# A Mamba-2 and ternary FFN kernel on one Trainium2 core: the total of a chunk's running sums comes from their last column by way of DRAM, and the sums from s on become a difference

## The chip, the cores and the metric

The kernel runs on one core of one Trainium2 chip. The metric is device time in microseconds. The kernel before took 1155.3 us, the median of three runs (1153.39 to 1156.26).

The engines work side by side, each in the order of its own instructions, and meet at semaphores: TensorE (PE; its weight loads are listed as PEld), VectorE (DVE), ScalarE (ACT), GpSimd (POOL) and SyncE (SP), which here only issues DMAs. PE multiplies a stationary operand (the weights) with a moving one and writes into PSUM; DVE and ACT read PSUM, DMAs and POOL work on SBUF.

## The reference

Sixteen sequences of 512 tokens with 256 features go through a Mamba-2 block and a feed-forward block with ternary weights, each with layer norms and residuals. The change touches the scan of the Mamba-2 block:

```python
dt = jax.nn.softplus(dt + dt_bias)
A = -jnp.exp(A_log)
dA = jnp.exp(dt * A)
xdt = xh * dt[..., None]
def step(S, inp):
    dA_t, xdt_t, B_t, C_t = inp
    S = dA_t[:, :, None, None] * S + xdt_t[..., None] * B_t[:, None, None, :]
    y_t = jnp.einsum('bhpn,bn->bhp', S, C_t)
    return (S, y_t)
_, y = lax.scan(step, S0, ...)
y = y.transpose(1, 0, 2, 3) + D[None, None, :, None] * xh
y = y.reshape(b, l, D_INNER)
y = y * jax.nn.silu(z)
y = y * lax.rsqrt(jnp.mean(y * y, axis=-1, keepdims=True) + 1e-05) * norm_w
return y @ out_proj_w.T
```

There are 8 heads of 64 values and a state of 128 for each value. The decay of a head over a stretch of tokens is the exponential of the sum of `a = dt * A` over them, so the scan can be cut into chunks once these sums are known.

## The kernel before

**Tiling.** A sequence is cut into 4 chunks of 128 tokens. 4 chunks times 8 heads give 32 columns, `W = 32`. `a` is a tile of 128 tokens x 32 columns.

**Stages of one sequence.** `stage_a` projects the input, does the convolution and the activations (`pm` on PE, L296; `cv` on ACT, L301, and DVE, L303; the silu, L308; `pz`, L318). `stage_a0` and `stage_t0` norm the input of a sequence ahead and transpose it to `x1T` (L273, L276). `stage_a2` computes softplus and `a` on DVE (L420 to L438) and calls `sums_of`. `stage_r` loads `mt` (the running sums of 8 heads, spread to all partitions), `stage_s` or, for three chunks of the first sequence, `stage_s_v` forms differences of running sums (ACT L538, DVE L525), `stage_b1` takes their exponentials (L549). `stage_b0` makes the decays `dec` and `ecum` (L473, L478), `stage_d` loads `ct` spread to all partitions, `stage_e` multiplies it by C (POOL L499). `stage_b2` walks over the chunks: `prepare` transposes x into `px` (L588), multiplies by dt (`xdt`, DVE L590), forms B C products (`pg`, L594 to L597), multiplies `mt` (L606) and makes `xend` on POOL (L603); then come the state `pst` (L623, L629), `py` (L637, L644) and `y` (L656, L660). `stage_c1` and `stage_c2` are the output projection (L709) and the feed-forward block (`ph` L755, gelu L761, `pf` L789, `o` L795).

**The sums.** `sums_of` makes, in one PSUM tile `pd`, three products on PE. `a` under the triangle `after` gives at token s the sum over the tokens after s in its chunk; `a` under `ones` gives the sum over the whole chunk, in every partition (both L449, outputs 128 x 32). `a` as weights against the triangle `incl` gives the running sums with the 32 columns as partitions and the tokens along the row (L450, output 32 x 128). ACT copies the running sums to `cum` (L454); DVE copies the other two to `sums` (L455), whose first half is the sum after s and second half the total. `cum` goes to DRAM as `raw` (L457) and comes back spread to all partitions as `mt` (L511). PE transposes `cum` (L461) and DVE copies that to `cums` (L463), token by token the running sum up to s. In `stage_b0`, later, ACT takes the exponential of all of `sums` in one instruction: `dec[:, 0]` weighs a token into the chunk's end state (L603), `dec[:, 1]` decays the old state over a chunk (L651).

**What sets the order.** On PE, ACT, POOL and DVE the order of the code is the order of the engine. The code is written as generators that `interleave` advances by hand-set shares. Each pass of the main loop has a first `interleave` (projections of sequence i + 1, first half of the block of i - 1) and a second one (feed-forward of i - 1, chunks of i, sums and decays of i + 1). In the second, `stage_a2(i + 1)` runs at 0.08 to 0.36, `stage_r` of two chunks at 0.365, `stage_b0(i + 1)` at 0.5. For the first sequence the stages are run one after the other:

```python
for stage in (
    stage_t0(1), stage_a6(0), stage_s_v(0, 1, 2, 3), ternary(1), stage_s(0, 0), stage_b0(0),
    stage_d(0), stage_b1(0, 0),
):
    run(stage)
```

`ternary(1)` rounds a weight matrix on DVE (L206). For the second sequence `stage_b0(1)` stands at 0.9 of a longer `interleave`. SP's DMAs are placed by the scheduler of the framework. Tiles are taken from pools with a fixed number of buffers: `pd` is in `ps_tr` (2 banks of PSUM), `sums` in `small` (3), DRAM tiles in `dram` (2). `ps_a` has 4 banks; its buffers go round `pm`, `pz`, `px`, `pst`, `py`.

Of the kernel before, what the change touches and what calls it, by code (L numbers as in the profile page):

```python
# [28 lines left out]
F32 = mybir.dt.float32  # L29
BF16 = mybir.dt.bfloat16  # L30
AF = mybir.ActivationFunctionType
ALU = mybir.AluOpType
# [3 lines left out]
P = 128  # L36
# [24 lines left out]
def mamba_ffn_kernel(  # L61
# [17 lines left out]
    nc = tc.nc  # L79
    NB = x.shape[0]  # L80

    const = ctx.enter_context(tc.tile_pool(name="const", bufs=1))
# [7 lines left out]
    dram = ctx.enter_context(tc.tile_pool(name="dram", bufs=2, space=bass.MemoryType.DRAM))  # L90
# [6 lines left out]
    def load_x(b):  # L97
# [9 lines left out]
    ones = const.tile([P, P], F32)  # L107
    nc.gpsimd.memset(ones, 1.0)
    incl = const.tile([P, P], F32)
    nc.gpsimd.affine_select(  # L110
        out=incl, in_=ones, compare_op=ALU.is_ge, fill=0.0, base=0,
        pattern=[[1, P]], channel_multiplier=-1,
    )
    after = const.tile([P, P], F32)
    nc.gpsimd.affine_select(
        out=after, in_=ones, compare_op=ALU.is_gt, fill=0.0, base=0,
        pattern=[[-1, P]], channel_multiplier=1,
    )
    mhalf = const.tile([P, NC], F32)
    nc.gpsimd.memset(mhalf, -0.5)  # L120
# [292 lines left out]
    def stage_a2(b):  # L413


        W = NC * NH
        dt, neg, sil = seqs[b]["dt"], seqs[b].pop("neg"), seqs[b].pop("sil")
        df = dt.rearrange("p c h -> p (c h)")
        z = small.tile([P, W], F32, tag="sp_z", name=f"sp_z_{b}", bufs=1)
        nc.vector.scalar_tensor_tensor(z, neg, 2.0, sil, ALU.mult, ALU.subtract)  # L420
        nc.vector.reciprocal(z, z)
        nc.vector.tensor_mul(z, z, sil)
        e = small.tile([P, W], F32, tag="sp_e", name=f"sp_e_{b}", bufs=1)
        nc.vector.tensor_mul(e, z, z)
        yield 0.15
        acc = small.tile([P, W], F32, tag="sp_a", name=f"sp_a_{b}", bufs=1)
        nc.vector.tensor_scalar_mul(acc, e, ATANH[0])
        for k in ATANH[1:3]:
            nc.vector.scalar_tensor_tensor(acc, acc, k, e, ALU.add, ALU.mult)
        yield 0.15  # L430
        for k in ATANH[3:]:
            nc.vector.scalar_tensor_tensor(acc, acc, k, e, ALU.add, ALU.mult)
        yield 0.15
        nc.vector.scalar_tensor_tensor(acc, acc, 1.0, z, ALU.add, ALU.mult)
        nc.vector.tensor_scalar_max(df, df, 0.0)
        nc.vector.scalar_tensor_tensor(df, acc, 2.0, df, ALU.mult, ALU.add)
        a = small.tile([P, NC, NH], F32, tag="a", name=f"a_{b}")
        nc.vector.tensor_tensor(a, dt, negA.unsqueeze(1).to_broadcast([P, NC, NH]), ALU.mult)  # L438
        yield 0.25
        yield from sums_of(b, a)  # L440

    def sums_of(b, a):


        W = NC * NH
        af = a.rearrange("p c h -> p (c h)")
        pd = ps_tr.tile([P, 512], F32, tag="tr", name=f"pd_{b}")
        for i, tri in enumerate((after, ones)):
            nc.tensor.matmul(pd[:, i * W : (i + 1) * W], tri, af, start=True, stop=True)  # L449
        nc.tensor.matmul(pd[0:W, 2 * W : 2 * W + P], af, incl, start=True, stop=True)  # L450
        sums = small.tile([P, 2, W], F32, tag="sums", name=f"sums_{b}")
        pc = pd[0:W, 2 * W : 2 * W + P]
        cum = small.tile([W, P], F32, tag="cum", name=f"cum_{b}", bufs=1)
        nc.scalar.copy(cum, pc)  # L454
        nc.vector.tensor_copy(sums.rearrange("p i w -> p (i w)"), pd[:, 0 : 2 * W])  # L455
        raw = dram.tile([W, P], F32, tag="raw", name=f"raw_{b}")
        nc.sync.dma_start(raw, cum)  # L457
        seqs[b].update(sums=sums, cum=cum, raw=raw)
        yield 0.15
        turned = pd[:, 2 * W + P : 3 * W + P]  # L460
        nc.tensor.transpose(turned, cum, ident[0:W, 0:W])  # L461
        cums = small.tile([P, W], F32, tag="cums", name=f"cums_{b}", bufs=2)
        nc.vector.tensor_copy(cums, turned)  # L463
        seqs[b].update(cums=cums)
        yield 0.15


    def stage_b0(b):


        s = seqs[b]
        s["dec"] = small.tile([P, 2, NC, NH], F32, tag="dec", name=f"dec_{b}")
        nc.scalar.activation(  # L473
            s["dec"].rearrange("p i c h -> p (i c h)"), s["sums"].rearrange("p i w -> p (i w)"),
            AF.Exp,
        )
        ecum = small.tile([NC * NH, P], F32, tag="ecum", name=f"ecum_{b}", bufs=1)
        nc.scalar.activation(ecum, s.pop("cum"), AF.Exp)  # L478
        s["way"] = dram.tile([NC * NH, P], F32, tag="way", name=f"way_{b}")
        nc.sync.dma_start(s["way"], ecum)  # L480
        yield 0.1
# [370 lines left out]
    with tc.manual_schedule(engines=ordered):  # L852
# [10 lines left out]
# [5 lines that stand above are left out]
# [13 lines left out]
            (stage_t0(2), T0_WORK, 0.81, 0.83),  # L881
            (stage_a6(1), 0.1, 0.84, 0.841),
            (stage_b0(1), 0.1, 0.9, 0.901),
            (stage_b1(1, 0, 1), 0.2, 0.902, 0.903),
            (stage_s(1, 2), 1.0, 0.92, 0.95),
# [3 lines left out]
        for i in range(1, NB - 1):  # L889
# [11 lines left out]
                (stage_r(i + 1, 0, 1), 0.2, 0.365, 0.37),  # L901
                (stage_s(i + 1, 0), 1.0, 0.44, 0.49),
                (stage_b0(i + 1), 0.1, 0.5, 0.51),
                (stage_b1(i + 1, 0), 0.1, 0.515, 0.52),
                (stage_s(i + 1, 1), 1.0, 0.53, 0.61),
# [70 lines left out]
```

## Time and profile before

| what | value |
|---|---|
| median of the runs | 1155.3 us |
| the profiled execution | 1156.0 us, of it the span of the instructions 1154.3 us |
| PE busy | 1090.4 us, 94% of the span |
| DVE, ACT, POOL busy | 824.8, 696.4, 588.9 us |
| granted TensorE clock | 0.977 of full speed on average |
| products L449 in the whole run | 64 instructions, 276 ns median each as the profile models them |
| copy of the sums L455 (DVE) | 16, 218 ns |
| `raw` to DRAM, `mt` back | 16 and 64 DMAs, 1.4 and 4.0 us to land |

The profile is one execution. Busy times of PE overlap in part, since matmuls are pipelined; the chain of waits, which follows the work that ended last back to the start, counts each stretch of time once. Its rows give start, length and what; those of the timeline give start, length, engine, line, operation and tiles, with the idle time before in brackets.

### The profile page before, as it was taken

What the parts mean: (1) busy time and instruction counts of PE and PEld (TensorE: products, weight loads), DVE (VectorE), ACT (ScalarE), POOL (GpSimd) and SP (SyncE); (2) the same over time, 40 slices, a digit from 0 to 9 for tenths busy, and PEclk for the clock granted to TensorE, in tenths of its full rate; (3) what the DMA queues carried; (4) which work ended last, traced back from release to release, by engine and by line L of the source; (5) the groups of instructions that cost most, each with busy time, mean ns of one, the idle gap of its engine ahead of it and who ended that gap; (6) DMA issues with size and microseconds to landing.
All of it is one profiled execution on the core that took longest, in us unless ns stands there. A gap on an engine that the chain in (4) does not pass through costs nothing.

```text
span 1154.3 us, 17172 instructions
## 1 busy us (share of the span) xinstructions
PE 1090.4 (94%) x6052; PEld 715.6 (62%) x6052; DVE 824.8 (71%) x2137; ACT 696.4 (60%) x1378; POOL 588.9 (51%) x699
## 2 busy tenths in 40 slices
PE   5787799999999999999999999999999999999897
PEld 2344367575766757576675757667575766757575
DVE  4674867769686776968677695867779586776652
ACT  5628465676666567666656766665675666566321
POOL 1243635646463564646356464635646463565842
PEclk9788899999999999999999999999999999999899
DMA  6312012220312222031222203122220312212000
GB/s 197 124 58 77 18 62 86 74 93 19 130 37 67 82 74 92 19 130 37 70 79 74 93 19 130 37 73 76 74 93 19 130 37 74 75 56 92 1 10 28
DMA packets 34534, 81.23 MB, mean 70 GB/s; under 512 B 4368, under 2 KB 23440, under 8 KB 32400
## 3 DMA queue, kind: packets, MB, share of 16 engines
q1 hardware_dynamic: 32896, 79.97, 20.0%
q8 instruction: 48, 0.79, 0.3%
q10 hardware_dynamic: 1552, 0.16, 0.1%
q14 instruction: 38, 0.31, 0.1%
HBM read 71.21 MB, written 8.91 MB: 69 GB/s over the span
## 4 chain that ended last, share of the span: by engine, by line
PE 56%; POOL 17%; DVE 15%; ACT 9%; issue 2%; DMA 1%; POOLq 0%; ACTq 0%; DVEq 0%
PE pf L789 19%; PE ph L755 12%; POOL ct L499 9%; PE py L637 5%; PE pm L296 5%; DVE cv L303 4%; PE pst L623 4%; ACT mt L538 4%; PE py L644 3%; POOL x3p L743 3%; DVE st_f L224 2%; DVE x L695 2%; ACT mt L549 2%; ACT cv L301 2%; POOL xend L603 1%
## 5 line engine op out<-in xcount | busy, mean ns | idle before, releaser
L303 DVE SCALAR_TENSOR_TENSOR cv<-pm,cw_sb,cv 128x511 f32<-128x511 f32 (+2 forms) x288 | 215.3, 748 | 75.5 <-ACT cv L301 68.3
L789 PE MATMUL pf<-w_sb,hT 128*128 128x256 f32 x1024 | 238.0, 382 | 0.0
L789 PEld LDWEIGHTS pf<-w_sb,hT 128*128 128x128 f32 x1024 | 190.0, 190 | 35.8 <-issue 11.5
L755 PE MATMUL ph<-x3p,w_bf 128*128 128x512 bf16 x768 | 190.5, 382 | 3.1 <-POOL x3p L743 0.7
L296 PE MATMUL pm<-x1T,win_sb 128*128 128x512 f32 x384 | 186.6, 609 | 0.3 <-ACT x1T L276 0.3
L761 ACT ACTIVATE hT<-ph,b_sb 128x512 f32<-128x512 f32 x128 | 88.0, 688 | 130.9 <-PE ph L755 130.7
L538 ACT ACTIVATE mt<-mt,cums 128x128 f32<-128x128 f32 x488 | 152.4, 388 | 0.0
L660 POOL TENSOR_TENSOR zs<-y,zs 128x512 f32<-128x512 f32 x64 | 81.4, 1272 | 108.2 <-DVE y L656 106.5
L709 PE MATMUL po<-wo_sb,zs 128*128 128x256 f32 x512 | 127.0, 393 | 4.1 <-DVE att L715 4.1
L755 PEld LDWEIGHTS <-w_bf 128*128 128x128 bf16 x768 | 70.8, 98 | 88.7 <-issue 24.1
L318 PE MATMUL pz<-x1T,win_sb 128*128 128x512 f32 x256 | 124.9, 611 | 0.7 <-ACT state L626 0.7
L709 PEld LDWEIGHTS po<-wo_sb,zs 128*128 128x128 f32 x512 | 96.9, 194 | 32.5 <-issue 14.3
L296 PEld LDWEIGHTS pm<-x1T,win_sb 128*128 128x128 f32 x384 | 71.1, 193 | 71.9 <-issue 66.1
L499 POOL TENSOR_TENSOR ct<-ct,xbc 128x1024 f32<-128x1024 f32 x48 | 113.1, 2383 | 0.0
L301 ACT ACTIVATE cv<-pm,cw_sb 128x512 f32<-128x512 f32 x96 | 65.1, 678 | 69.1 <-PE pm L296 67.8
L656 DVE SCALAR_TENSOR_TENSOR y<-xbc,dsk,py 128x128 f32<-128x128 f32 x256 | 71.3, 341 | 49.0 <-PE py L644 43.2
L568 POOL TENSOR_TENSOR y<-y 128x256 f32<-128x256 f32 x64 | 46.6, 728 | 115.3 <-ACT y L567 115.3
L637 PE MATMUL py<-mt,xdt 128*64 128x128 f32 x1024 | 95.7, 282 | 0.0
L322 ACT ACTIVATE zs<-pz 128x512 f32<-128x512 f32 x64 | 37.9, 592 | 86.4 <-PE pz L318 86.4
L231 POOL TENSOR_TENSOR rs_c<-rs_c,mhalf 128x2 f32<-128x2 f32 x32 | 25.1, 785 | 125.0 <-DVE rms L579 93.8
L318 PEld LDWEIGHTS pz<-x1T,win_sb 128*128 128x128 f32 x256 | 48.7, 196 | 58.0 <-issue 48.1
L644 PE MATMUL py<-ct,state 128*64 128x128 f32 x768 | 75.6, 276 | 6.9 <-POOL ct L499 6.9
(130 smaller groups left out, 1808.9 us busy)
## 6 DMA issues: line engine op xcount, KB each, us to landing
mt<-raw SPq DMA_DIRECT2D x64, 512.0 KB, 4.0
ct<-way SPq DMA_DIRECT2D x16, 1536.0 KB, 6.3
xin<-in_x SPq DMA_DIRECT2D x16, 512.0 KB, 3.8
out<-o SPq DMA_DIRECT2D x30, 256.0 KB, 2.2
w_in<-in_w SPq DMA_DIRECT2D x1, 1024.0 KB, 8.7
w_sb<-in_w SPq DMA_DIRECT2D x1, 1024.0 KB, 11.0
win_sb<-in_w_in SPq DMA_DIRECT2D x1, 768.0 KB, 6.0
win_sb<-in_w_in SPq DMA_DIRECT2D x1, 512.0 KB, 8.1
```

What stands on the lines that cost most here:

```text
L296: nc.tensor.matmul(pm, win_sb[:, k, DI + m * P : DI + (m + 1) * P], x1T[:, k, :], start=(k == 0), stop=(k == 1),)
L301: nc.scalar.activation(cv, pm, AF.Copy, scale=cw_sb[:, m, 3:4])
L303: nc.vector.scalar_tensor_tensor(cv[:, j:], pm[:, 0 : L - j], cw_sb[:, m, 3 - j : 4 - j], cv[:, j:], ALU.mult, ALU.add,)
L318: nc.tensor.matmul(pz, win_sb[:, k, j * P : (j + 1) * P], x1T[:, k, :], start=(k == 0), stop=(k == 1),)
L499: nc.gpsimd.tensor_tensor(ct[:, c - 1], ct[:, c - 1], xbc[:, 5, c * P : (c + 1) * P].unsqueeze(1).to_broadcast([P, NH, P]), ALU.mult,)
L538: nc.scalar.activation(mt[:, h, :], mt[:, h, :], AF.Relu, bias=s["cums"][:, c * NH + h : c * NH + h + 1], scale=-1.0,)
L637: nc.tensor.matmul(py[h % 2 * HD : (h % 2 + 1) * HD, j, :], xdt[:, h * HD : (h + 1) * HD], mts[c][:, h, :], start=True, stop=(c == 0),)
L644: nc.tensor.matmul(py[h % 2 * HD : (h % 2 + 1) * HD, j, :], state[:, h * HD : (h + 1) * HD], ct[:, c - 1, h, :], start=False, stop=True,)
L709: nc.tensor.matmul(po[:, 0:DM], g[:, k, c * P : (c + 1) * P], wo_sb[:, k, :], start=(k == 0), stop=(k == NJ - 1),)
L755: nc.tensor.matmul(ph, w1_bf[:, k, f * P : (f + 1) * P], x3p[:, j, k, :], start=(j == 0 and k == 0), stop=(j == 2 and k == 1),)
L761: nc.scalar.activation(hT[:, f, :], ph, AF.Gelu, bias=b1_sb[:, f : f + 1])
L789: nc.tensor.matmul(pf[:, 0:DM], hT[:, f, c * P : (c + 1) * P], w2_sb[:, f, :], start=(f == 0), stop=(f == NF - 1),)
```

## The change

The triangle `after` and the two products by `after` and `ones` go. The total of a chunk is the last entry of its running sums, so the last column of `cum` (32 values, one for each partition) is written to a DRAM tile `total`, ahead of `raw` on SP's queue. After the next `yield` it is read back as one row of 32 values, spread to all 128 partitions, into `sums[:, 1]`. In `stage_b0`, just ahead of the exponential, DVE forms `sums[:, 0]` as the total minus the running sum `cums`. The copy of the two products from PSUM goes; inside `pd` the remaining pieces move to the front.

```diff
-    after = const.tile([P, P], F32)
-    nc.gpsimd.affine_select(
-        out=after, in_=ones, compare_op=ALU.is_gt, fill=0.0, base=0,
-        pattern=[[-1, P]], channel_multiplier=1,
-    )
...
-        for i, tri in enumerate((after, ones)):
-            nc.tensor.matmul(pd[:, i * W : (i + 1) * W], tri, af, start=True, stop=True)
-        nc.tensor.matmul(pd[0:W, 2 * W : 2 * W + P], af, incl, start=True, stop=True)
+        nc.tensor.matmul(pd[0:W, 0:P], af, incl, start=True, stop=True)
         sums = small.tile([P, 2, W], F32, tag="sums", name=f"sums_{b}")
-        pc = pd[0:W, 2 * W : 2 * W + P]
+        pc = pd[0:W, 0:P]
         cum = small.tile([W, P], F32, tag="cum", name=f"cum_{b}", bufs=1)
         nc.scalar.copy(cum, pc)
-        nc.vector.tensor_copy(sums.rearrange("p i w -> p (i w)"), pd[:, 0 : 2 * W])
+        total = dram.tile([W, 1], F32, tag="total", name=f"total_{b}")
+        nc.sync.dma_start(total, cum[:, P - 1 : P])
         raw = dram.tile([W, P], F32, tag="raw", name=f"raw_{b}")
         nc.sync.dma_start(raw, cum)
         seqs[b].update(sums=sums, cum=cum, raw=raw)
         yield 0.15
-        turned = pd[:, 2 * W + P : 3 * W + P]
+        nc.sync.dma_start(
+            sums[:, 1, :], total.rearrange("w o -> (w o)").partition_broadcast(P)
+        )
+        turned = pd[:, P : W + P]
         nc.tensor.transpose(turned, cum, ident[0:W, 0:W])
         cums = small.tile([P, W], F32, tag="cums", name=f"cums_{b}", bufs=2)
         nc.vector.tensor_copy(cums, turned)
...
         s = seqs[b]
+        nc.vector.tensor_sub(s["sums"][:, 0, :], s["sums"][:, 1, :], s["cums"])
         s["dec"] = small.tile([P, 2, NC, NH], F32, tag="dec", name=f"dec_{b}")
         nc.scalar.activation(
             s["dec"].rearrange("p i c h -> p (i c h)"), s["sums"].rearrange("p i w -> p (i w)"),
```

## The prediction

> **What bounds the kernel.** I read the page first, then the chain of waits, then the timeline around the lines that the diff touches. The first row has the page's busy times, the second and third the busy tenths of TensorE (PE) and its granted clock in 40 slices, the fourth the chain's shares by engine, the last the DMA row of the running sums (size, us to landing).
>
> ```profile
> PE 1090.4 (94%) x6052; PEld 715.6 (62%) x6052; DVE 824.8 (71%) x2137; ACT 696.4 (60%) x1378; POOL 588.9 (51%) x699
> ...
> PE   5787799999999999999999999999999999999897
> ...
> PEclk9788899999999999999999999999999999999899
> ...
> PE 56%; POOL 17%; DVE 15%; ACT 9%; issue 2%; DMA 1%; POOLq 0%; ACTq 0%; DVEq 0%
> ...
> raw<-cum SPq DMA_DIRECT2D x16, 16.0 KB, 1.4
> ```
>
> PE is busy everywhere, but the chain is on it for only 56%. Passes repeat every 67.2 us (sums products L449 of two neighbouring sequences start at 624.75 and 691.95). In a pass the chain runs through ACT, DVE and POOL from about 590 to 617.5 and through PE from there to about 657, where the next pass begins. The chain in order of time, where the sums are formed in a steady pass (start, length, what):
>
> ```profile
> 624.58 0.22 PE pg L594 x2
> 624.81 0.11 PE pg L595
> 624.92 0.37 PE pd L449 x4
> 625.28 0.34 PE pd L450 x2
> 625.62 1.40 PE ph L755 x6
> 627.02 0.86 PE pst L623 x2
> 627.88 0.17 PE pd L461
> ```
>
> So the removed products lie on the path that sets the end. The same view of the start, first sequence:
>
> ```profile
> 31.21 1.06 PE pd L449 x4
> ...
> 49.50 1.28 ACT L473
> ...
> 51.16 1.04 ACT mt L549
> 52.20 0.57 ACT cv L301
> 52.76 2.85 ACT mt L549 x3
> ...
> 55.68 1.09 PE px L588 x4
> ```
>
> Here ACT is the path, and the first thing on it is the decay (L473), which the change makes wait for DVE.
>
> **1. Two sum products removed (gain).** A product by `after` or `ones` is two PE instructions, so four go for each sequence: 0.37 us in the row above. Timeline bounds: the first L449 starts at 624.75, the first L450 at 625.21, so at most 0.46 us; at least 0.30, the length of one pair of its weight loads. I take 0.37: the change to the 32-column weights of L450 stays and costs what it did. All 14 sequences from the third on show this pattern, PE has no wait in 617.5 to 654 but those for `xend` at its start and in step 2, and ACT, the next on the chain, sits idle 2.62 us for `pm` at 657.40, so an earlier PE is followed: 14 x 0.37 = 5.2 us. Second sequence: 0.56 us in the chain (78.48), I take 0.5. First: 1.06 us, but at half clock.
>
> Row against rule: before 40 us four matmuls L296 take 3.71 us, at 40.90 they take 1.72. The Trainium skill (TensorE: Matmul & The Clock Gate, Part 1: The HAM clock gate) says that the warm-up is a budget of time, windows of about 3.4 us, not of matmuls. By the row alone 1.06 us less cold work is 1.06 us gained. By the rule the clock rises at the same 40 us, and the pulled-in work is done cold instead of warm: 0.5 us. I take 0.5. Together 5.2 + 0.5 + 0.5 = 6.2 us.
>
> **2. The transposition L461 no longer waits for the copy of the sums (nothing).** The wait list names this copy:
>
> ```profile
> PEld pd L461 <- DVE sums L455: 10.6, 14, 0.8
> ```
>
> That looks like 0.76 us a pass. But the copy had ended at 627.18 (626.96 + 0.22), and PE was then in `pst`, until 627.72 (two of 0.43 from 626.86); the transposition starts at 627.81. At most 0.09 us can be gained, 14 x 0.09 = 1.3; it reads a weight tile of 32 rows as before, so I take 0 and keep 1.3 for the low end.
>
> **3. Two DMAs on SP's queue (nothing).** The write of `total` is issued ahead of `raw`, at 0.33 us per issue; its read, a broadcast of 128 bytes to each partition, stands ahead of the `mt` loads and holds SP until `total` has landed. ACT's `cum` copy comes 0.37 earlier, so `raw` still goes out near 625.94. No transfer this small is written in the trace; the nearest row is `raw`, 1.4 us (1.8 in the pass shown, 2.3 at most). Then `total`, out at 625.57, lands by 627.4, its broadcast is issued by 627.8, and the first `mt` load goes out at about 628.0 instead of 627.83. It takes 4.0 us, so it is there by 632.1; ACT wants it (L538) at 633.38 less 0.37. Cover left about 0.9 us. The broadcast lands by about 630, seven before its reader. Bounds: 0, and rival D if `total` is slow. Against the change speaks a rule of the skill (DMA: Bandwidth & Descriptors, Specifications): under 512 B the engines read, modify and write, and `total` is 4 bytes per partition. It gives no price; doubling 1.4 us eats 0.9 of cover at worst, so the sum is the same by row and rule.
>
> **4. DVE: copy (L455, 0.22 us) out, subtraction (0.19, by its nearest row, the 128x32 product L424) in, at L473's place.** Only the wait matters. In the order of the code the subtraction stands behind the last DVE work emitted before the decay. Steady pass and first sequence in the timeline:
>
> ```profile
> 635.83 1.28 ACT L473 ACT_TABLE_LOAD   x1
> 635.88 1.22 DVE L606 TENSOR_TENSOR mt<-mt,pg 128x1024 f32<-128x1024 f32 x1
> 637.12 0.26 ACT L473 ACTIVATE dec<-sums 128x64 f32<-128x64 f32 x1
> ```
>
> ```profile
> 50.58 2.73 DVE L206 SCALAR_TENSOR_TENSOR w_bf<-w_in,thalf 128x512 bf16<-128x512 f32 x4
> 50.79 0.26 ACT L473 ACTIVATE dec<-sums 128x64 f32<-128x64 f32 x1
> ```
>
> Steady: behind L606, which ends at 637.10. The subtraction ends near 637.29, so the decay is 0.2 us late; the table load covers the rest. Behind it on ACT: exponentials of `mt`, the copy of `pm` (640.70), for which DVE waits and then makes `y`, finally the copies of `x1T` (653.71), for which PE waits. ACT is idle 0.76 us for PE just before those copies, so 0.2 (with 0.5 more if `mt` came late) costs PE nothing. If the wait stood ahead of the table load, 1.28 us would be added: rival C.
>
> First sequence: behind all 24 L525 and the four L206, which end at 53.31. Subtraction until 53.42, decay at 53.46 instead of 50.79: ACT loses 2.67 us. Queued behind it: `ecum` and its DMA (`ct` is used only at 72.9, covered), L549, then L301 (52.10 to 54.77, done 55.43). DVE's L303 waits for that: 55.45 instead of 53.23, 2.2 late; it frees the buffer of PE's `px`, 55.68 to 57.9. From there the chain is serial, so I take 2.2 us lost; bounds 0 (something later absorbs it) and 2.7. The phase of PE's clock windows in the start may add or take up to 1 us.
> Second sequence: DVE's last work before it is L579, done at 101.14, and the decay starts at 102.99: nothing.
>
> **Sum.** -6.2 + 2.2 = -4.0 us. The profiled execution took 1156.0 us (span 1154.3), so 1152.0 on its scale; it is 0.7 above the median of the runs, 1155.3, from which 1151.3.
>
> **Rivals.**
> A, the above, 1151.3 (own range 1150.0 to 1153.0): 0.57.
> B, the stall of the start is not paid, or PE also gets the 0.09 of L461. For it: several cold and idle stretches up to 146 us could swallow 2 us. Against: the chain runs through this very ACT work. 1155.3 - 6.2 = 1149.1, down to 1147.8 with both: 0.17.
> C, the steady gain is not carried: PE meets another wait, or the decay's wait stands ahead of its table load (then ACT is 1.5 late, and less 0.76 and some 0.4 that PE's own work covers, PE loses the 0.37 it had gained; the start costs 3.5). Against: at 145.28 the load L761 ran first and its activation then waited 0.85 us for PE. 1155.3 - 1.0 + 2.2 = 1156.5, or 1157.8 with the load: 0.16.
> D, slower: `total` lands late, SP stands in its wait, and `mt` comes late. It decides from a landing of about 4 us: `mt` then lands near 633.9, beyond ACT's cover of 0.76 and the gain. At 6 us `mt` lands at 636.0, ACT is 3.2 late, PE 2.4, less 0.37: 14 x 2.0 + 1.2 = 29, so 1185. For it: the small loads of the start (`dtb`, `alog`) took 5.6 and 5.3 us to land. Against: those ran beside the weights (DMA busy 0.6 in that slice), `raw` in its own pass needs 1.4 to 2.3. 0.10.
>
> **Numbers.** 0.3% of 1155.3 is 3.5 us, about what a measurement can tell from no change: the border is 1151.8. Of A about 0.36 lies below it, of B nearly all: faster 0.52. The rest of A and C: same 0.38. D: slower 0.10. The range leaves out D and the lower half of B: 1149.0 to 1156.8, C's first form included.
>
> **What would show it.** Right: no L449; L450 about 0.2 us after L595; passes of 66.85 us instead of 67.2; an idle of ACT near 2.7 us before the first decay, named DVE sums, and about 0.2 before the later ones; no wait on L538 for DMA; L461 still about 0.5 us after the second `pst`. Wrong: passes of 67.2 (C) or above (D), the landing of `total` over 4 us, a table load behind the wait, or a first `px` near 55.7.

## The result, and the profile after

The changed kernel took 1183.4 us, the median of four runs (1179.7 to 1183.9), beside 1154.4 us for the kernel before: a ratio of 1.0247, 95% interval 1.0228 to 1.0266. It is 29 us slower, where 4 us faster had been forecast. Line numbers of the changed kernel: running sums L443, `cum` L447, write of `total` L449, `raw` L451, broadcast L454, transposition L458, subtraction L469, decay L471, load of `mt` L509, Relu L536.

The page of the changed kernel, busy times, busy tenths and granted clock of PE, the chain's shares by engine, and the DMA row of `mt`:

```profile
PE 1091.6 (92%) x5943; PEld 708.2 (60%) x5988; DVE 827.1 (70%) x2137; ACT 696.4 (59%) x1378; POOL 588.0 (50%) x698
...
PE   5687799999999999999999999999999999998897
...
PEclk9788899999999999999999999999999999999899
...
DVE 22%; PE 22%; POOL 21%; ACT 19%; DMA 12%; issue 3%; SPq 0%; POOLq 0%; ACTq 0%; DVEq 0%
...
mt<-raw SPq DMA_DIRECT2D x64, 512.0 KB, 5.9
```

The clock and every engine's busy time are within 0.3% of those before, but for PEld, which has fewer loads. What moved is the chain: PE's share fell from 56% to 22%, and DMA, which had 1%, has 12%, some 140 us. `mt` takes 5.9 us to land instead of 4.0. The list of DMAs, with the three small transfers (KB each, median us from issue to landing):

```profile
total<-cum SPq DMA_DIRECT2D x16, 0.1 KB, 4.1
raw<-cum SPq DMA_DIRECT2D x16, 16.0 KB, 4.7
sums<-total SPq DMA_DIRECT2D x16, 16.0 KB, 5.2
```

The write of 128 bytes takes 4.1 us, and `raw`, the same DMA as before, 4.7 instead of 1.4. The waits of the changed kernel (total us, times, longest):

```profile
ACT mt L536 <- DMA mt<-raw: 36.9, 12, 5.3
...
PEld pd L458 <- ACT hT L759: 10.6, 14, 0.8
```

The first is new. The second is the 10.6 us that stood before as the transposition's wait for the copy of the sums: the copy is gone, the wait stayed, under another name. Last the chain of a steady pass, from the running sums to the end of the stall:

```profile
637.20 0.35 PE pd L443 x2
...
637.58 0.26 ACT cum L447
...
637.85 0.33 SPq L449
...
638.24 5.62 DMA raw<-cum
...
643.87 3.80 DMA mt<-raw
...
647.76 0.24 ACT mt L536
...
651.52 0.26 ACT dec L471
...
655.20 0.58 ACT cv L296
...
667.46 0.48 ACT x1T L271
...
667.99 0.83 PE pss L573 x6
```

`raw` goes out at 638.24, right behind the write of `total`, and lands 5.62 us later. Of the last 14 passes, this is one of five in which `raw` lands some 6 us after `cum` and `mt` takes 3.8 to 5.0 us; in the other nine `raw` lands after 4.2 to 5.2 us and `mt`, behind the broadcast, takes 4.8 to 7.5. From there the chain is `mt`, ACT's Relu, exponentials, `cv` and, over DVE and POOL, the copies of `x1T`, for which PE waits: the way that the prediction had named for a late `mt`. Passes last 68.1 to 71.1 us instead of 67.2.

### The profile page after: what moved, and what is told of

Its sections match the earlier page's. It is cut to its first block, busy times and chain, and to the rows that moved or that the text cites. A ratio compares the mean times of both kernels' runs of the same rounds, so it can differ in the third digit from the quotient of the medians.

```text
span 1182.2 us, 17018 instructions
## 1 busy us (share of the span) xinstructions
PE 1091.6 (92%) x5943; PEld 708.2 (60%) x5988; DVE 827.1 (70%) x2137; ACT 696.4 (59%) x1378; POOL 588.0 (50%) x698
## 4 chain that ended last, share of the span: by engine, by line
DVE 22%; PE 22%; POOL 21%; ACT 19%; DMA 12%; issue 3%; SPq 0%; POOLq 0%; ACTq 0%; DVEq 0%
POOL ct L497 8%; ACT mt L536 8%; PE ph L753 7%; DVE cv L298 7%; DMA mt<-raw 6%; DMA raw<-cum 5%; PE pm L291 3%; PE pf L787 3%; ACT mt L547 3%; POOL x3p L741 3%; ACT cv L296 3%; DVE st_f L219 2%; DVE x L693 2%; DVE st_a L219 2%; PE py L635 2%
## 5 line engine op out<-in xcount | busy, mean ns | idle before, releaser
L787 PE MATMUL pf<-w_sb,hT 128*128 128x256 f32 x1024 | 242.2, 385 | 5.5 <-DVE o L793 5.5
L787 PEld LDWEIGHTS pf<-w_sb,hT 128*128 128x128 f32 x1024 | 190.3, 191 | 45.1 <-issue 11.5
L753 PE MATMUL ph<-x3p,w_bf 128*128 128x512 bf16 x723 | 185.1, 382 | 5.5 <-POOL x3p L741 0.6
L536 ACT ACTIVATE mt<-mt,cums 128x128 f32<-128x128 f32 x488 | 152.6, 387 | 44.3 <-DMA mt<-raw 36.9
```

The costliest lines, as they stand in the source:

```text
L536: nc.scalar.activation(mt[:, h, :], mt[:, h, :], AF.Relu, bias=s["cums"][:, c * NH + h : c * NH + h + 1], scale=-1.0,)
L753: nc.tensor.matmul(ph, w1_bf[:, k, f * P : (f + 1) * P], x3p[:, j, k, :], start=(j == 0 and k == 0), stop=(j == 2 and k == 1),)
L787: nc.tensor.matmul(pf[:, 0:DM], hT[:, f, c * P : (c + 1) * P], w2_sb[:, f, :], start=(f == 0), stop=(f == NF - 1),)
```

## The experiments

Each kernel is the changed one with the edit shown. Where the second half of `sums` no longer holds the total, the subtraction is also turned round, so that the values stay small, and the kernel does not compute what the reference does. Times are medians. The kernel before took 1154.8 to 1155.8 us beside them, and ratios are to it. "After `cum`" counts from the end of the copy of `cum` in the same pass. ACT wants the first `mt` of a pass 7.47 us after `cum`.

A later landing than that does not cost time at once. In the 13 steady intervals of the changed kernel and of the 13 others up to and with "The stall of the first sequence", a pass lasts 66.82 us plus what the first `mt` lands later than 8.5 us after `cum`, within 0.1 us: in the changed kernel a landing after 9.75 us goes with a pass of 68.07, one after 11.14 with 69.46, one after 12.76 with 71.14. Its 13 intervals lose 28.5 us, and the landings beyond 8.5 add up to 28.4. So the landing of this one load sets the loss, and the cover, the time by which it may come later at no cost, ends at 8.5 us; the 1.0 us from 7.47 on is taken up, in part at least, by ACT's wait for PE before the copies of `x1T`, which is 9.3 us in all without the two DMAs and 0.8 in the changed kernel.

### Neither DMA

```diff
+    held = [const.tile([P, 2, NC * NH], F32, name=f"held_{i}") for i in range(3)]
+    for t in held:
+        nc.gpsimd.memset(t, 0.0)
...
-        sums = small.tile([P, 2, W], F32, tag="sums", name=f"sums_{b}")
+        sums = held[b % 3]
-        total = dram.tile([W, 1], F32, tag="total", name=f"total_{b}")
-        nc.sync.dma_start(total, cum[:, P - 1 : P])
-        nc.sync.dma_start(
-            sums[:, 1, :], total.rearrange("w o -> (w o)").partition_broadcast(P)
-        )
```

> Both DMAs of total are left out; the second half of sums is zeros set once at the start and the difference is formed the other way round (running sum minus zero), so the decays are not the reference's; DVE, ACT and PE work is that of the changed kernel. Theory (the DMAs alone cost the time): raw lands in about 1.4 us, no wait of ACT for mt, passes of 66.85 us, total time about 1151 (1154.4 - 4.0 + noise). Rival (the subtraction on DVE and the decay's wait for it cost it): still above 1170, passes over 68.

1150.9 us (ratio 0.9957, 0.9942 to 0.9971). `raw` lands in 1.4 us, `mt` about 5.6 us after `cum`, ACT does not wait for it, and every steady pass takes 66.82 us. So the whole loss, 32 us, hangs on the two DMAs, and without them the time is that of the forecast, 1151.3 (not for all of its reasons, see below).

### The write alone, the read alone

The first keeps the write of `total` and drops only the broadcast (with `held` as above). The second drops the write and broadcasts from a tile that is written once at the start.

> As the kernel without the DMAs (decays not the reference's), but the 4-byte-per-partition write of total stays, ahead of raw; it is never read. Theory (the completion of the small write holds that of raw behind it): total lands in about 4 us, raw in 4 to 5 instead of 1.4, the first mt load goes out 5 us after cum instead of 1.5 and lands near 9 against a need at 7.5, passes about 1.2 us longer than without the DMAs, total time about 1167. Rivals (SP's wait for total, or the broadcast read, makes mt late): raw in 1.4 to 2.3 us and about 1151.

1159.1 us (1.0035, 1.0022 to 1.0049). A write that nobody reads costs 8 us against the run without it. Its DMA rows:

```profile
mt<-raw SPq DMA_DIRECT2D x64, 512.0 KB, 5.2
...
total<-cum SPq DMA_DIRECT2D x16, 0.1 KB, 3.3
raw<-cum SPq DMA_DIRECT2D x16, 16.0 KB, 3.7
```

`raw` lands 4.2 us after `cum` in nearly every pass, mostly some 0.8 us behind `total`. The packets show that the data itself is quick: in the pass at 155 us the 4-byte packets all start between 155.98 and 156.66, 7 to 9 ns each, and the 512-byte packets of `raw` in the same stretch, 25 to 34 ns each, yet the two land at 158.16 and 159.39. What is late is the completion.

The 8 us do not lie in every pass. In eight of the 13 steady ones `mt` lands 7.9 to 8.6 us after `cum`, at the end of the cover, and they lose 0.2 us at most. Five lose 1.0 to 2.1 us: there `raw` took 6.2 us, or the load of `mt` itself 5.3 to 6.2. In each of these five a fetch of the program's instructions (last section) starts 3.5 to 7.4 us after `cum`, as in only one of the other eight. So the write uses up the cover, and something else, perhaps these fetches, then shows.

> As the kernel without the DMAs (decays not the reference's), but the broadcast of total from DRAM stays, from a tile of zeros written once at the start. Theory (write): raw in 1.4 us, first mt load out at 1.5 to 2 us after cum, at most 1 us of delay in the landing of mt, which the 1.4 us of cover hides: about 1151 to 1153. Rival (the broadcast, 128 reads of the same 128 bytes, holds the mt load behind it): mt lands 5.9 us after its issue instead of 4.0, ACT waits, 1160 or more.

1154.9 us (1.0, 0.9988 to 1.0011), but this run told nothing of the read at its place: with nothing to wait for, the scheduler issued the broadcasts 200 us before their use in steady passes, far from `mt`. Steady passes took 66.83 us; the 4 us lie in the start.

### The broadcast at its place, without the write

```diff
-        total = dram.tile([W, 1], F32, tag="total", name=f"total_{b}")
-        nc.sync.dma_start(total, cum[:, P - 1 : P])
         nc.sync.dma_start(
-            sums[:, 1, :], total.rearrange("w o -> (w o)").partition_broadcast(P)
+            sums[:, 1, :], raw[0:1, 0:W].rearrange("o w -> (o w)").partition_broadcast(P)
         )
```

> The changed kernel without the write of total: the broadcast into the second half of sums stays at its place in SP's queue, ahead of the loads of mt, but reads 128 bytes of the first row of raw, so it waits for raw and for nothing else (the decay values are then not those of the reference; the subtraction is turned round so that they stay small). Theory 1 (the 4-byte write is the root: its late completion holds raw's): raw lands after 1.4 us again, the broadcast goes out about 1.5 us after the copy of cum and the first load of mt 0.4 us behind it, landing at most 1 us later than without the broadcast, which the cover of 0.9 us takes: 1150 to 1154 us. Theory 2 (the broadcast, 128 packets of 128 bytes from one place, standing ahead of mt, costs about half of the loss): mt lands 2 to 3 us later, ACT is idle 1.5 to 2.5 us before its first Relu in each pass, passes of about 67.8 us: 1163 to 1170 us.

1151.3 us (0.9976, 0.9965 to 0.9987). The broadcast takes 2.8 us, and the first `mt` behind it 5.3 us from issue instead of about 4.1, so it lands 7.2 us after `cum`: 1.6 us late, and hidden by the cover. One pass lost 0.9 us.

### `raw` ahead of `total`

```diff
+        raw = dram.tile([W, P], F32, tag="raw", name=f"raw_{b}")
+        nc.sync.dma_start(raw, cum)
         total = dram.tile([W, 1], F32, tag="total", name=f"total_{b}")
         nc.sync.dma_start(total, cum[:, P - 1 : P])
-        raw = dram.tile([W, P], F32, tag="raw", name=f"raw_{b}")
-        nc.sync.dma_start(raw, cum)
```

> The changed kernel with the two writes on SP in the other order, raw ahead of total. Theory (the completion of raw waits for the small write ahead of it): raw lands in 1.4 to 2 us; what is left is SP's wait for total (about 4 us after its issue, so the broadcast goes out at 4.5 and mt behind it at 4.9 after cum, landing 9 to 11): 1170 to 1180 if SP keeps the order of the code, 1152 to 1156 if its order lets the mt loads go first. If raw still lands in 4 to 6 us, the order of the two writes does not matter and the cause is another.

1167.3 us (1.0101, 1.0076 to 1.0125). `raw` lands in 1.4 us again, and the first load of `mt` is issued at 1.44, ahead of the broadcast. It still lands only 9.2 to 10 us after `cum`. In the pass at 837 us it is issued at 838.95; 8 of its 128 packets start before `total` lands at 842.75, and 115 from 844.0 on, 1.3 us and more after that. Half of them have started 5.9 us after the issue, against 2 us in the run without both DMAs. So the pending write also holds back the start of the reads behind it in the same queue. The order of the two writes is worth half of the loss, and is not its cause.

### What makes the write late: size, place or queue

Four runs with the write alone, changed in one thing each: whole rows of 512 bytes; 4 bytes, 512 bytes apart; 4 bytes, 64 bytes apart; and the original write, issued from ACT's queue.

All four replace these two lines:

```diff
-        total = dram.tile([W, 1], F32, tag="total", name=f"total_{b}")
-        nc.sync.dma_start(total, cum[:, P - 1 : P])
```

Rows:

```diff
+        total = dram.tile([W, P], F32, tag="total", name=f"total_{b}")
+        nc.sync.dma_start(total, cum)
```

> As the run with the write alone (1159.1 us, nothing reads what is written, the second half of the sums is zero), but the additional write ahead of raw takes the whole rows of cum, 512 bytes per partition, instead of the last column, 4 bytes. Theory 1 (the size of the pieces makes the write complete late): it lands after about 1.4 us, raw after 1.4 to 1.8, and the time falls to 1151 to 1153 us. Theory 2 (any second write to DRAM ahead of raw on this queue costs the same): raw lands after 3 us or more and the time stays at 1158 to 1160 us.

512 bytes apart:

```diff
+        total = dram.tile([W, P], F32, tag="total", name=f"total_{b}")
+        nc.sync.dma_start(total[:, P - 1 : P], cum[:, P - 1 : P])
```

> As the run with the write alone (1159.1 us, nothing reads what is written, the second half of the sums is zero), but the 32 values of 4 bytes go to places 512 bytes apart in DRAM instead of side by side. If the late completion comes from 32 writes into the same 128 bytes, one after the other, it goes: landing 1.4 to 2 us, 1151 to 1153 us. If it comes from each write being 4 bytes long, landing stays at 3 to 4 us and the time at 1157 to 1161 us.

64 bytes apart:

```diff
+        total = dram.tile([W, 16], F32, tag="total", name=f"total_{b}")
+        nc.sync.dma_start(total[:, 15:16], cum[:, P - 1 : P])
```

> As the run with the write alone, but with 64 bytes from each of the 32 values to the next (0 bytes between them gave landings of 3.0 to 4.1 us and 1159.1 us, 508 bytes between them 1.3 us and 1149.1 us). If the pieces collide only within 64 bytes: landing 1.3 to 1.5 us, 1149 to 1152 us. If they collide within 512 bytes, fewer to a block: landing between 1.6 and 4 us, 1152 to 1159 us.

From ACT's queue:

```diff
+        total = dram.tile([W, 1], F32, tag="total", name=f"total_{b}")
+        nc.scalar.dma_start(total, cum[:, P - 1 : P])
```

> As the run with the write alone (1159.1 us, nothing reads what is written, the second half of the sums is zero), but the 4-byte write is issued from ACT's queue, behind the copy of cum, instead of SP's. If its late completion holds back only what follows it in the same queue, raw lands after 1.4 us again and the time is 1151 to 1153 us (ACT's issue, some 0.1 to 0.3 us a pass, is covered by its idle time). If the hold lies in the DMA engines that both queues share, raw still lands after 3 us or more and the time is 1156 to 1160 us.

| write ahead of `raw` | `total` lands, median us | `raw` lands, median us | time us | ratio, 95% interval |
|---|---|---|---|---|
| 4 bytes side by side | 3.3 | 3.7 | 1159.1 | 1.0022 to 1.0049 |
| rows of 512 bytes | 1.4 | 1.5 | 1150.4 | 0.9955 to 0.9977 |
| 4 bytes, 512 apart | 1.3 | 1.5 | 1149.1 | 0.9942 to 0.9968 |
| 4 bytes, 64 apart | 1.3 | 1.5 | 1150.3 | 0.9942 to 0.9968 |
| side by side, from ACT's queue | 5.5 | 1.4 | 1150.7 | 0.9955 to 0.9977 |

The third row of the table in the DMA rows of its kernel:

```profile
total<-cum SPq DMA_DIRECT2D x16, 0.1 KB, 1.3
raw<-cum SPq DMA_DIRECT2D x16, 16.0 KB, 1.5
```

An additional write costs nothing, and a write of 4-byte pieces costs nothing. Late is only the one whose 32 pieces fall into the same 128 bytes; 64 bytes from piece to piece are enough. The packets of the late and the quick write look alike: with 512 bytes between the values they too start within 0.7 us, 7 to 9 ns each, and `total` lands 1.31 us after its issue in the same pass.

From ACT's queue the write is as late as ever, even later, but `raw`, issued at the same moment on SP's, isn't held. That does not tell the queue from the order, since the packets of `raw` start 0.07 us ahead of those of `total` there (555.75 and 555.82 in the pass at 555). The load of `mt` on SP's queue does tell: it goes out while the write on ACT's is pending. In 11 of the last 14 passes `total` lands some 4 us after that issue; by then at least 121 of the 128 packets of `mt` have started, half of them within 2 us, as without any write. Its completion is held all the same: it lands 0.45 us after `total` in 12 of 16 passes, some 0.6 us later than without any write, which is inside the cover. So in these runs the start of reads is held within a queue, and the completion across queues.

### Both DMAs, without the collision

Values 512 bytes apart and a broadcast of 128 bytes of `raw`: the two edits above together.

> The changed kernel with both DMAs at their places in SP's queue, but the write of total puts its 32 values 512 bytes apart, and the broadcast takes its 128 bytes from the first row of raw (the decay values are then not those of the reference). Theory 1 (the 32 writes of 4 bytes into the same 128 bytes are the cause, and write and read add up): total lands after 1.3 us, raw after 1.5, broadcast out at 1.9 and the first load of mt at 2.3 us after the copy of cum, landing at about 7.6: ACT idle 0 to 0.2 us, passes of 66.85 to 66.95 us, 1150.5 to 1153.5 us. Theory 2 (write and read together cost more than each alone also without the collision): passes of 67.5 us or more, 1160 us or more.

1155.5 us (1.0, 0.9992 to 1.0009). Landings are 1.3, 1.5 and 2.8 us, and in 10 of 13 steady intervals a pass takes 66.82 to 66.84 us. Three take 68.25, 67.67 and 68.04: there `raw` lands after 2.9 to 3.4 us, each time with an instruction fetch near (the last section), and the broadcast has used up the cover that hides this elsewhere. These three cost 3.5 us; the rest lies in the start, where the first `cum` came 1.5 us later than in the run without both, ahead of either DMA. So with both edits 28 of the 32 us are gone. One of them, the broadcast that reads `raw`, also changes what SP waits for; the next run has that one alone.

### Why write and read cost more together than one by one

Alone they cost 8 and 0.4 us, together 32. Either delays add over a cover, or the broadcast is slow because it reads bytes just written. This run keeps the colliding write and lets the broadcast read `raw`.

```diff
         nc.sync.dma_start(
-            sums[:, 1, :], total.rearrange("w o -> (w o)").partition_broadcast(P)
+            sums[:, 1, :], raw[0:1, 0:W].rearrange("o w -> (o w)").partition_broadcast(P)
         )
```

> The changed kernel with its 32 writes into the same 128 bytes ahead of raw, but the broadcast reads 128 bytes of raw instead of total (the decay values are then not those of the reference). Theory 1 (delays only add up: raw at 4.2 us after cum by the write, the broadcast 0.4 us of issue and 1.3 us on the first load of mt behind it): mt lands about 10 us after cum, ACT idle about 2.5 us, passes of 68.2 us and more, 1172 to 1182 us. Theory 2 (reading back the just written 128 bytes of total is itself slow, and holds SP's queue): without it mt lands at 8.5 to 9 us, 1160 to 1168 us.

1196.9 us (1.0355, 1.0336 to 1.0374), slower than both theories had it. It differs from the run before (1155.5 us) only in where the 32 values fall, so the collision is worth 41 us in this form.

```profile
mt<-raw SPq DMA_DIRECT2D x64, 512.0 KB, 5.9
...
total<-cum SPq DMA_DIRECT2D x16, 0.1 KB, 4.4
raw<-cum SPq DMA_DIRECT2D x16, 16.0 KB, 5.1
sums<-raw SPq DMA_DIRECT2D x16, 16.0 KB, 2.8
```

A slow read-back is not what the loss needs: without it the kernel gets slower, since the broadcast now waits for `raw` instead of `total` and the first `mt` goes out 0.4 us behind it. What adds up is seen in medians: `raw` 5.1 + 0.4 us after `cum` instead of 1.4, one issue of 0.4, and 5.6 us for `mt` behind the broadcast instead of 4.1. That is about 11.5 us after `cum`, 3 us beyond the cover's end at 8.5, and passes last 69.2 to 70.8 us. Up to a lateness of 2.9 us (8.5 less 5.6) nothing shows, so one delay hides and two don't. But the sum has a part that was in neither single run: `total` lands in 4.4 us here and in 4.1 in the changed kernel, against 3.3 in the write alone. Why the same 32 pieces complete later when a broadcast is in the program stays open.

The read-back is slow in the changed kernel, though: 5.2 us in its DMA row against 2.8 here. Its first packet starts 1.5 to 3.8 us after its issue, against 1.0 to 1.2 here, and in 11 of the last 14 passes the first `mt` lands 1.3 to 1.6 us behind it. It goes out there while `raw` is pending, here after `raw` has landed. Whether the pending write or the bytes just written make it late, no run separates.

### The whole change with 64 bytes between the values

```diff
-        total = dram.tile([W, 1], F32, tag="total", name=f"total_{b}")
-        nc.sync.dma_start(total, cum[:, P - 1 : P])
+        total = dram.tile([W, 16], F32, tag="total", name=f"total_{b}")
+        nc.sync.dma_start(total[:, 15:16], cum[:, P - 1 : P])
...
-            sums[:, 1, :], total.rearrange("w o -> (w o)").partition_broadcast(P)
+            sums[:, 1, :], total[:, 15:16].rearrange("w o -> (w o)").partition_broadcast(P)
```

> The whole change, with the 32 values of total 64 bytes apart in DRAM, so the broadcast reads 32 pieces of 4 bytes for each partition, 4096 in all, instead of 128 pieces of 128 bytes. Theory 1 (the collision of the writes is what costs): total lands after 1.3 us, and what remains is the broadcast ahead of mt: with 4096 pieces at 9 ns over 16 engines 2.3 us of transfer against 1.3 for the 128, so mt lands 1 us later than in the run with both DMAs and no collision (7.6 us after cum): 8.6 us, ACT idle about 1 us, passes of 66.9 to 67.3 us, 1157 to 1163 us. Theory 2 (4-byte reads cost much more each than 4-byte writes): mt lands beyond 10 us, 1170 us or more.

1184.9 us (1.0244, 1.0223 to 1.0265), no better than the change.

```profile
total<-cum SPq DMA_DIRECT2D x16, 0.1 KB, 1.3
raw<-cum SPq DMA_DIRECT2D x16, 16.0 KB, 1.5
sums<-total SPq DMA_DIRECT2D x16, 16.0 KB, 6.5
```

The write is quick now, and the read is slow: 4096 pieces of 4 bytes take 6.5 us, and the first `mt`, issued at 1.9, lands 10.6 us after `cum`. Sent from `cum`, where they stand in 32 partitions, the values are in small pieces on one side or the other. The last row of `cums`, the transposed sums, has the same 32 values side by side in one partition; a write from there was not run.

### The stall of the first sequence

Step 4 of the prediction took 2.2 us for ACT's wait before the first decay. This run is the one without both DMAs, with the first sequence's subtraction early.

```diff
         seqs[b].update(cums=cums)
+        if b == 0:
+            nc.vector.tensor_sub(sums[:, 0, :], cums, sums[:, 1, :])
...
-        nc.vector.tensor_sub(s["sums"][:, 0, :], s["cums"], s["sums"][:, 1, :])
+        if b > 0:
+            nc.vector.tensor_sub(s["sums"][:, 0, :], s["cums"], s["sums"][:, 1, :])
```

> As the run without both DMAs (1150.9 us, the second half of the sums zero), but the first sequence's subtraction stands directly behind the copy of cums, ahead of DVE's 24 operations on mt and the four on the weights; the other sequences are as before. Theory of step 4 (ACT's wait of 2.7 us before the first decay costs 2.2 us of the end): the wait goes, the first px starts 2.2 us earlier, 1148.7 us. Rival (something later in the start absorbs it): 1150 to 1151.5.

1150.8 us (0.9962, 0.995 to 0.9974), the same as with the stall. The timeline of PE in the run without both DMAs, with the stall:

```profile
56.78 1.08 PE L584 MATMUL px<-ident,xbc 128*128 128x128 f32 x4 [7.21 <-DVE cv L301]
...
61.08 1.98 PE L316 MATMUL pz<-x1T,win_sb 128*128 128x512 f32 x4 [0.68 <-ACT state L622]
```

The same of the run with the early subtraction:

```profile
53.93 1.09 PE L587 MATMUL px<-ident,xbc 128*128 128x128 f32 x4 [6.02 <-DVE cv L301]
...
58.38 3.78 PE L316 MATMUL pz<-x1T,win_sb 128*128 128x512 f32 x4 [0.67 <-ACT state L625]
```

Counted from the first running sums (31.05 and 31.19), `px` starts 25.73 and 22.74 us later: the stall is 3.0 us there. But the four `pz` behind it take 1.98 us with the stall and 3.78 without, and the 16 `py` after them 1.09 and 1.75: 2.5 of the 2.6 us that are given back. The windows of the run with the stall (from:to, length, PE busy, clock, DMA share, GB/s):

```profile
58.00:62.00 4.00, 3.33 (x8) 0.74 0.40 169
62.00:66.00 4.00, 4.00 (x25) 1.00 0.00 0
```

And without it:

```profile
58.00:62.00 4.00, 3.62 (x4) 0.50 0.00 0
62.00:66.00 4.00, 4.00 (x25) 0.82 0.00 0
```

After the idle stretch PE runs at half clock (0.50). If a stretch has half clock first and full clock then, its mean of 0.74 puts the change with the stall near 60.1, 3.3 us after `px` began; without the stall the mean of 0.82 puts it near 63.4, 9.5 us after. By the second sequence's sums (46.21 and 45.83 us after the first) 0.4 of the 3.0 us are left.

### The gain without a transfer

The decays exist elsewhere: the last column of `mt`, after its exponential, is exp(total - cum), and the last column of `ct`, before its product, is exp(total). So products, DMAs, subtraction and decay exponential can all go. Three placements of the copies. First those of `mt` on DVE and that of `ct` on POOL:

```diff
+            if c < NC - 1:
+                end = small.tile([P, NH], F32, tag="end", name=f"end_{n}")
+                nc.vector.tensor_copy(end, mts[c][:, :, P - 1])
...
+            nc.gpsimd.tensor_copy(s["dec"], s["ct"][:, 0 : NC - 2, :, P - 1])
```

> Neither the sums products nor the two DMAs nor the subtraction: the decay factors are taken from tiles that exist anyway. exp(total - cum) is the last column of mt after its exponential, copied by DVE ahead of the product that overwrites it (three copies of 128x8 a pass); exp(total) is the last column of ct, copied by POOL ahead of its first product. The copy of the sums on DVE, the subtraction and the decay exponential on ACT are gone, so the first sequence has no wait of ACT for DVE. Theory 1 (steps 1, 2 and 4 of the prediction): -6.2 us of step 1 and nothing for the stall, 1155.1 - 6.2 = 1148.9, within 1147 to 1151. Rival (the small copies or POOL's wait for ct cost a pass 0.2 us or more on the way from px to pst): 1152 to 1155.

1159.7 us (1.0038, 1.0026 to 1.005), passes of 67.46 us: slower than before. DVE's copies of `mt` (min/median/max in ns):

```profile
L581 DVE COPY end<-mt x48: 162/165/1062, 55.2 to 1079.6; 128x8 f32<-128x8 f32 x48
```

And the chain of a pass of the same kernel:

```profile
614.91 0.94 DVE end L581
615.86 0.59 DVE xdt L586
```

A copy of 0.16 us took 1.03 us here, from 614.83 on. In this pass POOL had begun two products for `x3p` (2.29 us for both) at 614.67. The 48 copies divide by POOL alone: 33 begin with no POOL instruction under way and take 0.16 to 0.17 us; 15 begin while one runs (14 of them one of `x3p`), and each ends 0.03 us after POOL's, 0.42 to 1.06 us long. So the copy waits for POOL's instruction to end. That agrees with the Trainium skill (Trainium Architecture — The Big Picture, What this means for kernel authors), by which DVE and GpSimd lock each other out of a port pair that they share.

Next, those of `mt` on ACT, each behind its exponential:

```diff
+                nc.scalar.copy(end, mt[:, :, P - 1])
```

> As the run that takes the decay factors from the last columns of mt and ct (1159.7 us), but ACT makes the three copies of the last column of mt, each directly behind the exponential that fills it, instead of DVE ahead of the product that overwrites it. Theory 1 (DVE's copy of 128x8, 0.94 us instead of 0.16 on the chain while POOL works on x3p, is the 0.63 us by which a pass was too long there): passes of 66.8 us or less again, 1148 to 1151 us. Rival (the three copies delay ACT on its way to the copies of x1T, or the missing decay step shifts other work): passes of 67.0 us or more, 1153 us or more.

1153.8 us (0.9986, 0.9976 to 0.9996), passes of 67.11 us. The chain there goes over POOL's copy:

```profile
605.03 0.15 POOL dec L483
605.18 0.07 issue
605.25 7.03 POOL ct L492 x3
```

Last, that of `ct` on ACT too, in a stretch where ACT is idle:

```diff
+            nc.scalar.copy(s["dec"], s["ct"][:, 0 : NC - 2, :, P - 1])
```

> As the run that takes the decay factors from the last columns of mt and ct with ACT's copies of mt (1153.8 us), but ACT also makes the copy of the last column of ct, in its idle stretch after the fourth mt of a pass, instead of POOL ahead of its three ct products. Theory 1 (POOL's products of ct are on the chain there, and its copy, 0.15 us with 0.07 us of issue, and the products, 7.03 instead of 6.97 us, are the 0.29 us by which a pass of 67.11 us is longer than one of 66.82): passes of 66.8 us, 14 x 0.29 = 4 us less, 1149 to 1151 us. Rival (the three copies of mt on ACT are the cause): passes of 67.0 us or more, 1152 us or more.

1151.0 us (0.9958, 0.9945 to 0.9972), passes of 66.82 us, and this kernel computes what the reference does. The chain has `POOL ct` with no copy ahead of it (6.98 us). This version is 0.4% faster than the kernel before and beats the changed one by 32 us. A copy of 0.16 us on an idle engine is free; on the engine that the chain goes through it costs its length and more.

## Why the prediction was wrong, point by point

**Step 1 (two products, -6.2 us): right in the steady passes.** They take 66.82 us in the run without both DMAs, against 67.2: 0.38 us, where 0.37 was taken. The 1.0 us of the first two sequences cannot be told from the stall.

**Step 2 (the transposition, nothing): right.** The wait of 10.6 us in 14 passes is still there, as gelu's.

**Step 3 (two DMAs, nothing): wrong, and this is the step that failed.** It took 1.4 us for `total`, by the row of `raw`; it landed after 4.1. The row was near in kind and size of transfer, but not in where the pieces fall: those of `raw` are 512 bytes apart, those of `total` share 128 bytes, and that, not their length, is what the runs separate. The second error was to let only SP's wait for `total` reach `mt`, and to take `raw` as unchanged: `raw` itself went from 1.4 to 4.7 us behind the write, and the first `mt` went out 5.2 us after `cum` instead of 1.5. Against this stood a rule that the prediction didn't weigh. The Trainium skill (DMA: Bandwidth & Descriptors, Queues, rings and completion order) says that a DMA's semaphore increment lands only after every earlier write of that DMA engine, across its queues; `raw` landing 0.8 us behind `total` in the run with the write alone, and `mt` on SP's queue 0.45 us behind `total` on ACT's, are what it describes. The rule that was weighed, read-modify-write under 512 bytes, does not give the price by the length of the pieces: 4-byte pieces with 64 bytes from one to the next land in 1.3 us. Whether it is what makes pieces in the same 128 bytes slow, no run shows. The third error was to give the broadcast no price: it costs the `mt` behind it 1.2 to 1.5 us, which alone is hidden and here wasn't, and reading back `total` it took 5.2 us itself. All this put the first `mt` at 10.4 us after `cum` (median), where the prediction had 6.6.

**Step 4 (the subtraction): mechanism right, its price wrong.** ACT's idle before the first decay is there, 2.45 us in the changed kernel (2.67 forecast), and in steady passes 0.13 us without the DMAs (0.2 forecast). "From there the chain is serial, so I take 2.2 us lost" did not hold: taking the stall away makes `px` 3.0 us earlier and the next sums 0.4 us. The phase of PE's clock, put at up to 1 us, gave back 2.6.

**The sum.** Steps 1, 2 and 4 alone give -3.9 us by the medians, -3.3 to -6.7 by the ratio's interval; -4.0 was forecast. That the two agree is in part luck: in the profiled executions the steady passes gain 5.0 us, as forecast, but the times from the first to the second `cum` and from there to the third change by -0.57 and +0.52 us, together nothing, where the prediction had +1.2. The start's own differences from run to run (1.5 us at the first `cum`) are too large to say more.

**Rival D (slower, 0.10) is what happened,** at 1183 against its 1185, though by another link: not SP standing in `total`'s wait alone, but `raw` completing late and `mt` behind the broadcast. Its step from `mt` to the time was right: `mt` at 633.9, 8.4 us after `cum`, as the limit (measured 8.5), and at 636.0, 10.5 us after it, for 1185 (measured 10.4 for 1183). Its step from `total` to `mt` was not: it needed a landing of 6 us for that, and 4.1 were enough. At 4.1 its own reckoning would have given next to no loss; that it came so near with 1185 is luck. Its evidence against, "`raw` in its own pass needs 1.4 to 2.3", was the same wrong row. B's first half, a stall that isn't paid, also came true, unseen under the loss.

## What to carry to other kernels

A DMA's landing is read from a row that is like it in where its pieces fall in DRAM too; a column written side by side is not like a tile written in rows. Ask of a new DMA not only who waits for it but what follows it: in these runs the DMAs behind completed after it, and a load that was just in time is late by the sum of all these delays less one cover. Before a small value goes through DRAM, look for it in a tile that is in SBUF anyway, and put the copy on an engine that the chain doesn't go through.

## What the runs showed of the hardware that was not expected

- 32 writes of 4 bytes into the same 128 bytes of DRAM complete 3.0 to 4.8 us after issue (up to 6.1 with `raw` ahead), with 64 bytes or more from one to the next in 1.3 us (median). The packets themselves take 7 to 9 ns each in both cases.
- A pending write of this kind delays the completion of DMAs behind it, also on another queue (`mt` on SP's lands 0.45 us after `total` on ACT's), and the start of reads behind it in its own queue (`raw` ahead of `total`: 115 of 128 packets of `mt` start 1.3 us or more after `total` has landed).
- Reading 128 bytes into each of 128 partitions takes 2.8 us, the same 128 bytes in 4-byte pieces 6.5 us, and 128 bytes just written in 4-byte pieces, with `raw` pending, 5.2 us.
- A copy of 0.16 us on DVE that begins while POOL is in an instruction ends 0.03 us after that instruction, in 15 of 15 cases.
- `raw` lands late in some passes of kernels without any new DMA. The trace has the fetches of the program's own instructions, packets of 16 KB of 0.9 to 1.5 us each. Their queue in the page of the run without both DMAs (packets, MB, share):

```profile
q8 instruction: 47, 0.77, 0.3%
```

  Beside five issues of `raw` in the trace of that run:

```
raw issued   landing us   16 KB instruction packet: start after raw's issue, length
221.09       2.54         0.01   1.45
287.91       3.19         0.98   1.18
354.73       3.46         1.03   1.25
421.53       1.40         1.45   0.92
621.98       1.40         5.85   0.98
```

  In this run the passes where such a packet starts within 0.4 us before or 1.4 us after the issue of `raw` are those where `raw` takes 2.5 to 3.5 us, in the kernel before too (1.8 to 2.3). In other runs a few packets between 1.2 and 1.5 us after the issue leave `raw` at 1.4 us, and a few late landings have none so near. That one causes the other was not tested. Where these packets fall differs from kernel to kernel, so an edit may move them onto a transfer that has no cover.
